# Reciprocal roots of three layer normalisations: a power on POOL in place of a guessed start and Newton steps

## The chip, the cores and the metric

The kernel runs on one core of a Trainium2 chip. The metric is the device time of one execution in microseconds. The kernel before was run three times: median 2804.71 us, lowest 2804.29, highest 2805.34.

## The reference

A decoder layer in fp32 on x of shape (2, 2048, 512): three sublayers, each a layer normalisation followed by a residual branch.

```python
def _layernorm(x, axis=-1, eps=1e-05):
    m = jnp.mean(x, axis=axis, keepdims=True)
    v = jnp.var(x, axis=axis, keepdims=True)
    return (x - m) / jnp.sqrt(v + eps)

x = x + attn(_layernorm(x), W_q, W_k, W_v, W_o)   # 16 heads of 32, rotary positions, softmax
h = gelu(_layernorm(x) @ ctx^T)                    # ctx_1024: 77 rows of 512, per batch
x = x + h @ ctx
w = (weights >= 0) * 2 - 1                         # 512 x 512
x = x + clip((_layernorm(x) @ w^T) * scale + bias, -100, 100)
```

What matters here is `1 / sqrt(v + eps)`: one number per row of x and per normalisation, 3 x 4096 in all. In the kernel a row lies on a partition, so for one chunk of 128 rows it is a tile of one column.

## The kernel before

A batch has 2048 rows: 16 chunks of 128 rows, or 4 blocks of 4 chunks. Each of the two batches goes through two stages.

**Projection** (`project_batch`, L153). For each chunk: `norm` computes mean and variance on DVE (`chunk_stats`: bn_stats L129, bn_aggr L130 into the tile mv), the reciprocal root, and on ACT the scaled chunk xn = x * rstd + off (L168) with off = -mean * rstd. `turn` transposes xn on PE (pt, L174) and copies it to xnt on ACT (L176). PE then multiplies xnt with the three weights (pk, pq, pv, all L181), DVE and POOL rotate k and q (L209 to L214; the last addition of r is POOL's), and PE transposes them (ptqk, L189). The normalisation of chunk ch + 1 is written ahead of the products of chunk ch. Input chunks and weights come by DMA from the SP queue (L71, L76).

**Attention** (`Attention.run`, L595). A batch has 32 units (a block of queries, a group of four heads, a half block), and a unit 8 steps. In each half of a step PE computes scores (st, L516) and, for a unit ahead, scores for the row maxima (ps, L423); ACT takes the exponential (pw, L643); POOL adds two halves of it (sm, L645); DVE reduces the maxima (L435). PE weighs the values (acc, L534) one step later and sums sm with a matrix of ones (acc, L548) two steps later. In this stage the order on PE, DVE, ACT and POOL is the order of the program (`tc.manual_schedule`); elsewhere a planner orders the instructions of each engine. After a unit's last step ACT copies acc to num (L562), DVE takes a reciprocal (L568) and a product gives the attention output (L571), which overwrites q.

**After attention** (`after_attention`, L284) is a generator that handles 4, 2 or 1 chunks of a block ("a piece"): output projection (po, L329) and residual addition on DVE (L298), a normalisation, the context branch (ph L336, the gelu steps L341 to L350, po L355), a second normalisation, and the last branch (pf, L363, then y: L365 on DVE, L367 to L370 on POOL) and the store (L372). Every `yield` ends one slot. Pieces stand in a first-in first-out queue. `background` (L380) runs one slot after one half of every second step and after the second half of every step (L654, L663); in the last four units of a batch it runs one in each half (L652). During the next projection it runs three at a time, and `drain` empties the queue before that projection's last block. When all attention is done, the rest runs alone (`alone` is set), one slot of each piece in turn.

**The normalisation** is in both places three parts. `rstd_seed` (L133) makes v = var + eps on DVE and a first guess of the root by shifting and subtracting the bits as an integer (L138, L139). `rstd_step` (L144) is one Newton iteration of four dependent small instructions (L145 to L148), run three times on POOL. Then two instructions make off (L165, L166 or L311, L312). Inside `after_attention` the iterations and off go to `side()`, which is POOL, or DVE once the kernel is alone; a slot ends after the seed, after each iteration and, twice, after off. In `project_batch` there are no slots. The small tiles (mv, v, rstd, t, off) have two buffers each (pool `small`, L63).

The lines that the change touches and those that call them:

Of the kernel before, what the change touches and what calls it, by code (L numbers as in the profile page):

```python
# [8 lines left out]

F32 = mybir.dt.float32  # L10
BF16 = mybir.dt.bfloat16
U32 = mybir.dt.uint32
I32 = mybir.dt.int32
AF = mybir.ActivationFunctionType
ALU = mybir.AluOpType
AX = mybir.AxisListType

P = 128
# [6 lines left out]
CPB = BLK // P  # L25
# [6 lines left out]
EPS = 1e-5  # L32
# [5 lines left out]
def decoder_layer(  # L38
# [16 lines left out]
    nc = tc.nc  # L55

    const = ctx.enter_context(tc.tile_pool(name="const", bufs=1))
# [5 lines left out]
    small = ctx.enter_context(tc.tile_pool(name="small", bufs=2))  # L63
# [31 lines left out]
    nc.vector.memset(ones_b, 1.0)  # L95
    ones = const.tile([P, DK], F32, tag="ones", name="ones")
    nc.vector.memset(ones, 1.0)


    mts = []  # L100
# [26 lines left out]
    def chunk_stats(xc, mv):  # L127
        st = small.tile([P, 6], F32, tag="st", name="st")
        nc.vector.bn_stats(st, xc)  # L129
        nc.vector.bn_aggr(mv, st)  # L130


    def rstd_seed(var, n):  # L133
        v = small.tile([P, n], F32, tag=f"v{n}", name="v")
        nc.vector.tensor_scalar(v, var, 1.0, EPS, ALU.mult, ALU.add)
        y = small.tile([P, n], F32, tag=f"rstd{n}", name="rstd")
        t = small.tile([P, n], F32, tag=f"t{n}", name="t")
        nc.vector.tensor_scalar(t.bitcast(I32), v.bitcast(I32), 1, None, ALU.arith_shift_right)  # L138
        nc.vector.tensor_scalar(  # L139
            y.bitcast(I32), t.bitcast(I32), -1.0, float(0x5F3759DF), ALU.mult, ALU.add  # L140
        )
        return v, y, t

    def rstd_step(engine, v, y, t):  # L144
        engine.tensor_mul(t, y, y)  # L145
        engine.tensor_mul(t, t, v)
        engine.tensor_scalar(t, t, -0.5, 1.5, ALU.mult, ALU.add)
        engine.tensor_mul(y, y, t)  # L148

# [1 line left out]
    def project_batch(b, ahead, att, wk, wq, wv):  # L153

        def norm(ch):
            xc = ahead.pop(0)
            if ch + 2 < NCH:
                ahead.append(load_x(b, ch + 2))
            mv = small.tile([P, 2], F32, tag="mv1", name="mv")
            chunk_stats(xc, mv)  # L160
            v, y, t = rstd_seed(mv[:, 1:2], 1)
            for _ in range(3):
                rstd_step(nc.gpsimd, v, y, t)
            off = small.tile([P, 1], F32, tag="off1", name="off1")
            nc.gpsimd.tensor_mul(off, mv[:, 0:1], y)  # L165
            nc.gpsimd.tensor_scalar(off, off, -1.0, None, ALU.mult)  # L166
            xn = work.tile([P, D], F32, tag="w", name="xn")
            nc.scalar.activation(xn, xc, AF.Identity, bias=off, scale=y)  # L168
            return xn

        def turn(xn):
            pt = ps_t.tile([P, ND, P], F32, tag="t", name="pt")
            for i in range(ND):
                nc.tensor.transpose(pt[:, i, :], xn[:, i * P : (i + 1) * P], ident)  # L174
            xnt = work.tile([P, ND, P], F32, tag="w", name="xnt")
            nc.scalar.copy(xnt, pt)  # L176
            return xnt

        def times(dst, xnt, w, part=range(ND)):
            for i in part:  # L180
                nc.tensor.matmul(dst, xnt[:, i, :], w[:, i, :], start=(i == 0), stop=(i == ND - 1))  # L181

        def transpose_qk(ch, qk, which=(0, 1)):
            blk, c = divmod(ch, CPB)
            cols = slice(c * P, (c + 1) * P)
            for a in which:
                pt = ps_s.tile([P, ND, P], F32, tag="s", name="ptqk")
                for i in range(ND):
                    nc.tensor.transpose(pt[:, i, :], qk[:, a, i * P : (i + 1) * P], ident)  # L189
                (nc.vector.tensor_copy if a else nc.scalar.copy)((att.q, att.k)[a][blk][:, :, cols], pt)  # L190
            if c == CPB - 1 and 1 in which:
                att.open_block(blk)

        def values(ch, xnt, pool=None):
            pv = (pool or ps_s).tile([P, D], F32, tag="t" if pool else "s", name="pv")
            times(pv, xnt, wv)
            v = kvq.tile([P, D], F32, tag=f"v{ch}", name=f"v_{b}_{ch}")
            nc.scalar.copy(v, pv)  # L198
            att.v.append(v)


        def rotate(ch, a, ps, r):
            half = [P, H, DK // 2]
            cs = cos[:, ch, None, :, None].to_broadcast(half + [2])
            sn = sin[:, ch, None, :].to_broadcast(half)
            pairs = ps.rearrange("p (h i t) -> p h i t", i=DK // 2, t=2)
            t1 = r[:, 0, a, :].rearrange("p (h i t) -> p h i t", i=DK // 2, t=2)
            t2 = r[:, 1, a, :].rearrange("p (h i t) -> p h i t", i=DK // 2, t=2)
            nc.vector.tensor_tensor(t1, pairs, cs, ALU.mult)  # L209
            nc.vector.scalar_tensor_tensor(  # L210
                t2[:, :, :, 0], pairs[:, :, :, 1], -1.0, sn, ALU.mult, ALU.mult
            )
            nc.vector.tensor_tensor(t2[:, :, :, 1], pairs[:, :, :, 0], sn, ALU.mult)  # L213
            nc.gpsimd.tensor_add(r[:, 0, a], r[:, 0, a], r[:, 1, a])  # L214

        xnt = turn(norm(0))
        held = None
        for ch in range(NCH):
            if ch == (NB - 1) * CPB:
                drain()  # L220
            blk, c = divmod(ch, CPB)
            if c == 0:
                att.q.append(kvq.tile([P, ND, BLK], F32, tag=f"q{blk}", name=f"q_{b}_{blk}"))
                att.k.append(kvq.tile([P, ND, BLK], F32, tag=f"k{blk}", name=f"k_{b}_{blk}"))
            r = big.tile([P, 2, 2, D], F32, tag="s", name="r")
            xn = norm(ch + 1) if ch + 1 < NCH else None
            pk = ps_t.tile([P, D], F32, tag="t", name="pk")
            pq = ps_t.tile([P, D], F32, tag="t", name="pq")
            if ch == NCH - 1:
                break  # L230
            times(pk, xnt, wk)
            rotate(ch, 1, pk, r)
            att.lead(1)
            background(3)
            times(pq, xnt, wq)
            rotate(ch, 0, pq, r)
            if held is not None:
                transpose_qk(*held)
            held = (ch, r[:, 0])
            xnt_next = turn(xn)  # L240
            if ch < NCH - 2:
                values(ch, xnt)
            else:
                left = xnt
            att.lead(1)
            background(3)
            xnt = xnt_next


        times(pk, xnt, wk)  # L250
        rotate(ch, 1, pk, r)
        transpose_qk(*held)
        values(ch - 1, left, ps_t)
        transpose_qk(ch, r[:, 0], (1,))
        for i in range(ND):
            times(pq, xnt, wq, (i,))
            att.lead(1)
        rotate(ch, 0, pq, r)
        att.lead(2 * AHEAD)
        values(ch, xnt, ps_t)  # L260
        transpose_qk(ch, r[:, 0], (0,))
        att.split_maxima(0)
        att.turn_maxima(0)
        att.key_steps()
# [5 lines left out]
    def side():  # L270
        return nc.vector if alone else nc.gpsimd
# [12 lines left out]
    def after_attention(b, blk, ot, first, end):  # L284
        wo, wf, fs, fb = late["wo"], late["wf"], late["fs"], late["fb"]
        ctxn, ctxt = late["ctx"]
        n = end - first
# [14 lines left out]


        def norm(mv):
            v, y, t = rstd_seed(mv[:, :, 1], n)
            yield False
            for _ in range(3):
                rstd_step(side(), v, y, t)
                yield False
            off = small.tile([P, n], F32, tag=f"off{n}", name="off")  # L310
            side().tensor_mul(off, mv[:, :, 0], y)  # L311
            side().tensor_scalar(off, off, -1.0, None, ALU.mult)  # L312
            yield False
            yield False
            for c in range(n):
                xn = work.tile([P, D], F32, tag="w", name="xn2")
                nc.scalar.activation(
                    xn, xs[c], AF.Identity, bias=off[:, c : c + 1], scale=y[:, c : c + 1]
                )
                yield True  # L320
                pt = bank([P, ND, P], "pt2")
                for i in range(ND):
                    nc.tensor.transpose(pt[:, i, :], xn[:, i * P : (i + 1) * P], ident)  # L323
                nc.scalar.copy(ot[:, :, chunks[c]], pt)
                yield c + 1 == n
# [5 lines left out]
        mv = small.tile([P, n, 2], F32, tag=f"mv{n}", name="mv2")  # L331
# [25 lines left out]
        mv = small.tile([P, n, 2], F32, tag=f"mv{n}", name="mv3")  # L357
# [375 lines left out]
```

## Time and profile before

| what | us |
|---|---|
| median of three runs | 2804.71 |
| the profiled execution, its own time | 2803.13 |
| its span | 2801.0 |
| PE busy (matmuls) | 2762.5 |
| POOL busy | 1804.3 |
| DVE busy | 1714.5 |
| ACT busy | 1319.9 |
| PE matmuls on the chain that ended last | 96% of the span |

The span runs from the first to the last instruction of one profiled execution. Busy times of different engines overlap. The 2.1 us between the span and that execution's own time lie around the span. In the stages: the first projection lasts until about 228 us, the first attention until 1368, the second projection until about 1620, the second attention until 2752, and what runs alone until 2801.

### The profile page before, as it was taken

The numbers are of one execution on the slowest core, as the hardware profiler recorded it, in microseconds if no ns is written. First come the engines' busy times: TensorE is split into PE (matmuls) and PEld (weight loads), VectorE is DVE, ScalarE is ACT, GpSimd is POOL, SyncE is SP. The second block draws the span as 40 slices with busy tenths as digits, with TensorE's granted clock in tenths as the row PEclk, the third lists the DMA queues.
The fourth block names the chain that finished last, engine by engine and source line by source line (L and its number), as shares of the span: only waits on it lengthen the run. The fifth ranks groups of instructions, "written<-read, shape, count | busy, mean of one in ns | idle before, by whom it ended". The sixth has DMA issues, their size and how long they took to land.

```text
span 2801.0 us, 70846 instructions
## 1 busy us (share of the span) xinstructions
PE 2762.5 (99%) x30748; PEld 1490.8 (53%) x30748; DVE 1714.5 (61%) x3003; ACT 1319.9 (47%) x2391; POOL 1804.3 (64%) x2393
## 2 busy tenths in 40 slices
PE   8999999999999999999999999999999999999997
PEld 4445555555555555555444455555555555555553
DVE  4436777666666766665244467766766666666644
ACT  1114555455546544654322155555555455545542
POOL 4326767567757685767644287766777566857772
PEclk9999999999999999999999999999999999999998
DMA  4000000000100010000201000000000000000000
GB/s 136 20 19 2 5 4 4 4 4 7 30 3 4 4 33 4 4 4 33 72 24 31 15 4 4 4 4 4 4 17 20 4 4 11 26 4 4 18 11 16
DMA packets 41864, 43.56 MB, mean 16 GB/s; under 512 B 24759, under 2 KB 24759, under 8 KB 41553
## 3 DMA queue, kind: packets, MB, share of 16 engines
q1 hardware_dynamic: 41552, 39.05, 4.7%
q8 instruction: 240, 3.93, 0.6%
q14 instruction: 72, 0.58, 0.1%
HBM read 26.58 MB, written 8.39 MB: 12 GB/s over the span
## 4 chain that ended last, share of the span: by engine, by line
PE 96%; DVE 2%; POOL 1%; issue 1%; ACT 0%; DMA 0%; ACTq 0%; DVEq 0%; POOLq 0%
PE st L516 21%; PE acc L534 21%; PE ps L423 18%; PE acc L548 8%; PE pf L363 4%; PE pk L181 4%; PE po L329 4%; PE pv L181 4%; PE pq L181 4%; PE st L501 3%; PE pt L323 1%; PE po L355 1%; PE ph L336 1%; PE ptqk L189 1%; PE pt L174 1%
## 5 line engine op out<-in xcount | busy, mean ns | idle before, releaser
L645 POOL TENSOR_TENSOR sm<-pw 128x512 f32<-128x512 f32 x1024 | 1297.6, 1271 | 628.4 <-ACT pw L643 624.2
L435 DVE TENSOR_REDUCE mx<-ps 128x1 f32<-128x512 f32 x2048 | 1311.8, 682 | 566.6 <-PE ps L423 563.9
L643 ACT ACTIVATE pw<-st 128x512 f32<-128x512 f32 x2048 | 1111.3, 595 | 1004.0 <-PE ps L423 665.9
L423 PE MATMUL ps<-k,q 32*128 32x512 f32 x4096 | 1221.6, 639 | 2.2 <-ACT v L198 1.1
L534 PE MATMUL acc<-pw,v 128*32 128x256 f32 x8192 | 655.6, 391 | 0.0
L548 PE MATMUL acc<-sm,ones 128*32 128x128 f32 x7680 | 392.2, 280 | 1.4 <-POOL sm L645 1.4
L423 PEld LDWEIGHTS ps<-k,q 32*128 32x128 f32 x4096 | 359.4, 183 | 46.7 <-issue 24.3
L534 PEld LDWEIGHTS acc<-pw,v 128*32 128x32 f32 x8192 | 162.4, 108 | 402.3 <-issue 383.2
L548 PEld LDWEIGHTS acc<-sm,ones 128*32 128x32 f32 x7680 | 248.7, 110 | 157.2 <-POOL sm L645 2.7
L516 PE MATMUL st<-q,dkq 32*128 32x256 f32 x2048 | 291.4, 401 | 0.0
L516 PE MATMUL st<-q,dkk 32*128 32x256 f32 x2048 | 291.0, 400 | 0.0
L516 PE MATMUL st<-q,dkv 32*128 32x256 f32 x2048 | 289.9, 400 | 0.0
L516 PE MATMUL st<-q,k 32*128 32x256 f32 x2048 | 265.5, 375 | 0.0
L516 PEld LDWEIGHTS st<-q,dkk 32*128 32x128 f32 x2048 | 175.4, 184 | 90.1 <-issue 48.0
L516 PEld LDWEIGHTS st<-q,dkq 32*128 32x128 f32 x2048 | 172.2, 184 | 79.9 <-issue 55.2
L516 PEld LDWEIGHTS st<-q,dkv 32*128 32x128 f32 x2048 | 174.7, 184 | 68.8 <-issue 37.3
L516 PEld LDWEIGHTS st<-q,k 32*128 32x128 f32 x2048 | 194.4, 187 | 13.6
L214 POOL TENSOR_TENSOR r<-r 128x512 f32<-128x512 f32 x64 | 81.0, 1267 | 184.6 <-DVE r L213 167.0
L568 DVE RECIPROCAL num<-num 128x128 f32<-128x128 f32 x128 | 120.5, 943 | 64.2 <-ACT num L562 64.2
L190 ACT COPY q<-ptqk 128x512 f32<-128x512 f32 x32 | 18.9, 590 | 222.6 <-PE ptqk L189 222.6
L181 PE MATMUL pk<-wk,xnt 128*128 128x512 f32 x256 | 119.7, 611 | 2.7 <-ACT xnt L176 2.7
L363 PE MATMUL pf<-wf,q 128*128 128x512 f32 x256 | 119.1, 609 | 0.0
(99 smaller groups left out, 1963.9 us busy)
## 6 DMA issues: line engine op xcount, KB each, us to landing
x<-in_x_dram SPq DMA_DIRECT2D x64, 256.0 KB, 2.7
out_dram<-x SPq DMA_DIRECT2D x32, 256.0 KB, 2.0
wk<-in_wk_t_dram SPq DMA_DIRECT2D x2, 1024.0 KB, 5.3
wq<-in_wq_t_dram SPq DMA_DIRECT2D x2, 1024.0 KB, 8.0
wv<-in_wv_t_dram SPq DMA_DIRECT2D x2, 1024.0 KB, 12.9
wo<-in_wo_t_dram SPq DMA_DIRECT2D x1, 1024.0 KB, 7.0
wf<-in_wf_t_dram SPq DMA_DIRECT2D x1, 1024.0 KB, 9.1
mrow<-mt SPq DMA_TRANSPOSE x62, 2.3
```

What stands on the lines that cost most here:

```text
L181: nc.tensor.matmul(dst, xnt[:, i, :], w[:, i, :], start=(i == 0), stop=(i == ND - 1))
L329: nc.tensor.matmul(ps, ot[:, i, cols], wo[:, i, :], start=(i == 0), stop=(i == ND - 1))
L363: nc.tensor.matmul(pf, ot[:, i, cols], wf[:, i, :], start=(i == 0), stop=(i == ND - 1))
L423: nc.tensor.matmul(ps, self.q[qb][self.rows[h], g, q0 : q0 + P], self.k[kb][self.rows[h], g, :], start=True, stop=True,)
L435: nc.vector.tensor_reduce(mx[:, qc, h, kb : kb + 1], ps, AX.X, ALU.max)
L501: nc.tensor.matmul(self.st[h], ones_b[r, :], mrow[r, None, :].to_broadcast([DK, 2, HQ]), start=True, stop=False, skip_group_check=True,)
L516: nc.tensor.matmul(self.st[h][:, c, :], keys[r, g, kc * P : (kc + 1) * P], self.q[qb][r, g, hf * HQ : (hf + 1) * HQ], start=False, stop=Tr ...
L534: nc.tensor.matmul(acc[self.rows[h], 0, :], self.v[self.chunk(i, c)][:, d0 : d0 + DK], pw[:, h, c, :], start=(i == 0 and c == 0), stop=(i ...
L548: nc.tensor.matmul(acc[self.rows[h], 1, part], ones, sm[:, h, part], start=False, stop=(i == STEPS - 1), skip_group_check=True,)
L568: nc.vector.reciprocal(num[:, 1, part], num[:, 1, part])
L643: nc.scalar.activation(pw[:, h], self.st[h], AF.Exp, scale=SCALE)
L645: nc.gpsimd.tensor_add(sm[:, hs, :], pw[:, hs, 0, :], pw[:, hs, 1, :])
```

## The change

The seed and the three Newton iterations go. The new helper `scale_and_shift` adds eps on the given engine, raises the sum to the power -0.5 on POOL with a constant tile of -0.5, and makes off on the given engine as before. Both `norm` functions call it: the projection with POOL; the pieces with `side()`, so with POOL, or with DVE around the one POOL instruction once the kernel is alone. In a piece all of it is in one slot, followed by the two yields that stood after off. For one normalisation that leaves 4 small instructions of 17, and 2 slots of 6.

```diff
+    minus_half = const.tile([P, CPB], F32, tag="minus_half", name="minus_half")
+    nc.vector.memset(minus_half, -0.5)
...
-    def rstd_seed(var, n):
-        v = small.tile([P, n], F32, tag=f"v{n}", name="v")
-        nc.vector.tensor_scalar(v, var, 1.0, EPS, ALU.mult, ALU.add)
+    def scale_and_shift(engine, mv, n):
         y = small.tile([P, n], F32, tag=f"rstd{n}", name="rstd")
-        t = small.tile([P, n], F32, tag=f"t{n}", name="t")
-        nc.vector.tensor_scalar(t.bitcast(I32), v.bitcast(I32), 1, None, ALU.arith_shift_right)
-        nc.vector.tensor_scalar(
-            y.bitcast(I32), t.bitcast(I32), -1.0, float(0x5F3759DF), ALU.mult, ALU.add
-        )
-        return v, y, t
-
-    def rstd_step(engine, v, y, t):
-        engine.tensor_mul(t, y, y)
-        engine.tensor_mul(t, t, v)
-        engine.tensor_scalar(t, t, -0.5, 1.5, ALU.mult, ALU.add)
-        engine.tensor_mul(y, y, t)
+        engine.tensor_scalar(y, mv[:, :, 1], EPS, None, ALU.add)
+        nc.gpsimd.tensor_tensor(y, y, minus_half[:, :n], ALU.pow)
+        off = small.tile([P, n], F32, tag=f"off{n}", name="off")
+        engine.tensor_mul(off, mv[:, :, 0], y)
+        engine.tensor_scalar(off, off, -1.0, None, ALU.mult)
+        return y, off
...
-            mv = small.tile([P, 2], F32, tag="mv1", name="mv")
-            chunk_stats(xc, mv)
-            v, y, t = rstd_seed(mv[:, 1:2], 1)
-            for _ in range(3):
-                rstd_step(nc.gpsimd, v, y, t)
-            off = small.tile([P, 1], F32, tag="off1", name="off1")
-            nc.gpsimd.tensor_mul(off, mv[:, 0:1], y)
-            nc.gpsimd.tensor_scalar(off, off, -1.0, None, ALU.mult)
+            mv = small.tile([P, 1, 2], F32, tag="mv1", name="mv")
+            chunk_stats(xc, mv[:, 0])
+            y, off = scale_and_shift(nc.gpsimd, mv, 1)
...
         def norm(mv):
-            v, y, t = rstd_seed(mv[:, :, 1], n)
-            yield False
-            for _ in range(3):
-                rstd_step(side(), v, y, t)
-                yield False
-            off = small.tile([P, n], F32, tag=f"off{n}", name="off")
-            side().tensor_mul(off, mv[:, :, 0], y)
-            side().tensor_scalar(off, off, -1.0, None, ALU.mult)
+            y, off = scale_and_shift(side(), mv, n)
             yield False
             yield False
```

More of the change, by code (lines that the diff above doesn't have):

```diff
@@ L11 @@
 BF16 = mybir.dt.bfloat16
-U32 = mybir.dt.uint32
-I32 = mybir.dt.int32
 AF = mybir.ActivationFunctionType
```

## The prediction

> **What bounds the kernel now.** I read the page's head first, then a table of busy time by stage, TensorE's waits, the chain at both ends, and the groups of the instructions concerned.
>
> ```profile
> span 2801.0 us, 70846 instructions
> PE 2762.5 (99%) x30748; PEld 1490.8 (53%) x30748; DVE 1714.5 (61%) x3003; ACT 1319.9 (47%) x2391; POOL 1804.3 (64%) x2393
> ```
>
> PE is busy 2762.5 of 2801.0 us. No arithmetic of PE changes, so the change can only move the 38.5 us in which PE is idle, the matmuls at half clock, or POOL far enough to become the bound. By stage (length, then each engine's busy us):
>
> ```profile
> 0.00:11.00 11.00, 0.26 (x1) 0.26 (x2) 2.83 (x15) 2.10 (x2) 4.89 (x34) 1.00 0.80 248
> 230.00:1340.00 1110.00, 1109.73 (x14286) 616.25 (x14284) 737.52 (x1189) 596.79 (x1090) 785.18 (x879) 1.00 0.03 9
> 1340.00:1372.00 32.00, 27.66 (x335) 15.90 (x326) 7.26 (x25) 17.23 (x31) 23.85 (x61) 1.00 0.33 108
> 1372.00:1620.00 248.00, 244.03 (x797) 113.59 (x797) 104.64 (x247) 46.97 (x78) 108.20 (x281) 1.00 0.09 26
> 2751.60:2801.00 49.40, 32.26 (x88) 15.23 (x88) 28.00 (x110) 7.57 (x14) 0.00 (x0) 0.82 0.06 21
> ```
>
> PE's idle time sits at the start (10.7), between the batches (4.3), in the second projection (4.0) and after the last attention (17.1); attention itself leaves 0.3. What PE waits for:
>
> ```profile
> PE pt L174 <- ACT xn L168: 13.2, 3, 10.7
> PE pt L323 <- ACT xn L317: 8.7, 3, 5.6
> ```
>
> Both are the scaled chunk, the last link of a normalisation. The chain at the start (start, us, what):
>
> ```profile
> 4.37 0.18 DVE mv L130
> ...
> 9.88 0.82 ACT xn L168
> ...
> 12.53 6.49 PE pk L181 x8
> ```
>
> and at the end, where two one-chunk pieces, A and B, run side by side:
>
> ```profile
> 2755.59 3.45 PE po L329 x8
> ...
> 2764.41 0.17 DVE mv L130
> ...
> 2769.75 0.82 ACT xn L317
> ...
> 2780.72 0.17 DVE mv L130
> ...
> 2783.93 0.82 ACT xn L317
> ```
>
> The removed steps, of which L145 stands for four lines:
>
> ```profile
> L145 POOL TENSOR_TENSOR t<-rstd x150: 187/194/207, 5.7 to 2741.7; 128x1 f32<-128x1 f32 x96, 128x4 f32<-128x4 f32 x36, 128x2 f32<-128x2 f32 x18
> L145 DVE TENSOR_TENSOR t<-rstd x12: 151/159/160, 2761.3 to 2783.0; 128x1 f32<-128x1 f32 x12
> ```
>
> **What the Trainium skill says.** GPSIMD Engine Reference, Performance pitfalls: a chain of dependent fp32 operations costs 4 cycles a step at 1.2 GHz; its Specifications give each of eight cores 16 lanes and 16 partitions, so one column of a tile is one vector. No page prices the power, and no row of the trace has one. Perfetto Trace Analysis, GPSIMD Engine Instruction: POOL's times are better read from start to start. Here L145 lasts 0.19 but dependent steps are 0.27 apart; I use 0.27 on POOL and 0.19 on DVE. TensorE: Matmul & The Clock Gate, Part 1: TensorE starts at half clock; the trace agrees (first pk 6.49 us, later ones 3.43).
>
> **Cost of the power.** From below: any small two-input step, 0.27 us. Estimate from the skill's 4 cycles: a logarithm and an exponential of about 50 dependent steps (my assumption) are 200 cycles, 0.17 us a column; with the fixed 0.27 about 0.5 for one column and 1.0 for four. From above: the 16 lanes one after another, 16 x 0.17 = 2.6 us a column, 10.6 for four. I take 0.5 and 1.0. The range keeps both ends.
>
> **The change, part by part.** (1) *Start.* The aggregate ends at 4.55. Then a 0.09 hop, add 0.27, power 0.5, product 0.27, negation 0.26: ACT starts at 5.9 instead of 9.88, and pk could start at 8.6. But wk must have landed. wq was issued at 2.11 and took 10.9 us (13.0), wv 2.66 and 12.9 (15.6), so 2.6 us per weight matrix, and wk about 10.4. Gain 12.53 - 10.4 = 2.1 (0 to 3.9). If wk was early, the whole 3.9 shows.
>
> (2) *Attention.* 12 normalisations of four columns and 6 of two run on POOL. Each loses 3 DVE seeds and 12 POOL steps of 0.27 and gets an add, a power and the same two last steps, all in one slot. That slot is 0.27 + 1.0 + 0.27 + 0.27 = 1.8 us where three had 1.1 each and a fourth 0.5. Queued behind it are the sm additions (L645), for which PE's row sums wait; but a step's sums are taken two steps later, and a step is (1368.2 - 227.6) / 256 = 4.46 us. This slack hides it: 0. DVE's seeds were hidden as well. POOL's add now waits for DVE's aggregate, given a slot (about 2 us) before it: 0.
>
> (3) *Between batches.* POOL runs the first two normalisations of the second batch between the last sm additions (1348 to 1354), then a piece's L145-L148 steps; from 1351 to 1361 the chain alternates between sm and these steps, and PE waits. Of the 4.34 us idle, 2.1 (pt L174 for xn, then pk for xnt) stand behind the last num copy and stay; of the other 2.2 I take 2.0.
>
> (4) *Second projection.* PE idles 1.10 in 1415-1420 and 1.58 in 1465-1470, where POOL is busy 4.75 and 3.92 of 5 us with interleaved Newton steps. 16 instead of 48 steps there: 2.0 of the 2.7. The rest of the 4.0 also stands in the first projection, and stays. DVE's waits for a free mv (68.9 us, 21 times) shrink; PE covers them. The wait for a free rstd passes from DVE (10.3 us) to POOL's add, with the r additions behind it: covered.
>
> (5) *Tail.* Every normalisation also loses four yields. The queue is first in, first out, so the last four-chunk piece ends 8 slots sooner and the two-chunk piece after it (queued near 2600.7, begun at 2672.2) 16 sooner. It overhung attention by 7 slots (pt, pf, pf and their y steps), so all of it moves inside. PE is full there: +0.44 + 2 x 3.44 = +7.3. In return, from the end of the last acc (2751.6): po starts when the first q is divided (2753.6), not at 2755.4: 1.8. B's addition no longer waits for DVE (2762.46 to 2762.94): 0.5. B's first normalisation, aggregate to ACT, is 5.2 now, as it is interleaved with A's 17 steps and y; it becomes 0.19 + 0.1 + 0.5 + 0.1 + 2 x 0.19 = 1.3: 3.9. The second 3.0 becomes 1.3: 1.7. And A, one po (3.4) ahead of B, can run its pf under B's normalisation; I take half: 1.7. Net 9.6 - 7.3 = 2.3.
>
> Sum 2.1 + 2.0 + 2.0 + 2.3 = 8.4. The profiled execution took 2803.1 (span 2801.0 and 2.1 around it): 2794.7. The runs' median is 1.6 above it: 2804.7 - 8.4 = 2796.3.
>
> **Rivals.** *Covered:* wk lands only just before 12.5, A and B stay coupled, and the gaps of (3) and (4) half remain: 0 + 1 + 1 + 0.6, so 2802. For it: the landing of wk isn't shown, and the moved 7.3 us nearly cancel the tail. Against it: several independent gaps would all have to stay. *The first power loads its code:* GPSIMD Engine Reference, Instruction dispatch, has about 6 us for the first call of a freshly loaded kernel. Here it would fall on the start's chain: ACT at about 11.9, 2.0 later than now, total 8.4 - 2.1 - 2.0 = 4.3, 2800. Nothing in the trace speaks to it. *POOL becomes the bound (slower):* with lanes in turn a four-column slot holds POOL 10.6 + 0.8 us against 4.5 of slack: 12 x 6.9 + 6 x 1.6 = 92 us of PE waiting in L548 for sm; start and tail lose 3 x 2.1 of their gain. About 2804.7 + 92 - 2 = 2895. It decides from about 4.3 us for four columns, where 12 x (4.3 + 0.8 - 4.5) = 7 eats the sum. Against it: vector lanes; for it: no measured power. *The change does nothing* can't be: the tail's chain is DVE steps that vanish.
>
> **How the numbers follow.** Forecast 0.68 (own range 2792 to 2801), covered 0.09, code load 0.04, POOL bound 0.19 (anything from 2806 to 2900). About 0.2% (5.6 us) is what can be told from no change: the bounds are 2799.1 and 2810.3. Nine tenths of the forecast is faster, 0.61; its rest, the two middle cases and the cheapest of the slow end 0.20; slower 0.19. 0.05 lie below 2790 and 0.14 above 2822.
>
> **What would show it.** The power's row on POOL: under 1.2 us for four columns, (2) holds; over 4, idle PE at L548. Start: pk's first matmul near 10.4. 1340-1372: PE idle near 2.3. The last two-chunk piece's pf before the last acc, po 2 us after it, and from last acc to the end about 37 us instead of 46.4. It is wrong if POOL's power is several microseconds, or if the shifted pieces meet another full engine (y on POOL is 4.5 us a chunk) inside attention.

## The result, and the profile after

The changed kernel takes 2784.42 us (median of six runs, 2783.80 to 2785.53) against 2804.68 for the kernel before in its six (2803.58 to 2805.34): a ratio of 0.9928, 95% interval 0.9916 to 0.9941. That is 20.3 us less where 8.4 were forecast, and below the range of 2790 to 2822. The direction and several terms of the sum held; one term priced at nothing was the largest of all, and one priced as a gain was a loss.

The head of the page, kernel after:

```profile
span 2782.8 us, 70154 instructions
PE 2750.7 (99%) x30748; PEld 1491.3 (54%) x30748; DVE 1675.7 (60%) x2792; ACT 1320.4 (47%) x2391; POOL 1756.4 (63%) x1903
```

PE runs the same 30748 matmuls, yet its busy time fell from 2762.5 to 2750.7 us. So 11.8 of the 18.2 us of span were lying inside time that the page had counted as busy. Idle time fell only from 38.5 to 32.1. This is the first thing that the prediction's reading ("the change can only move the 38.5 us in which PE is idle", the matmuls at half clock, or POOL) left out. Half clock isn't where the 11.8 were: the stretches with a granted clock of 0.50, the start aside, sum to 20.4 us before and to 23.1 after.

Busy time by stage, kernel after (stretch, length, then busy us of PE, PEld, DVE, ACT, POOL with instruction counts, granted clock, DMA share, GB/s):

```profile
0.00:11.00 11.00, 2.25 (x6) 1.33 (x7) 2.24 (x10) 3.39 (x4) 2.91 (x14) 1.00 0.75 253
230.00:1340.00 1110.00, 1109.00 (x14329) 619.55 (x14326) 730.02 (x1172) 599.91 (x1095) 782.96 (x823) 1.00 0.03 9
1340.00:1372.00 32.00, 29.93 (x283) 16.10 (x284) 3.44 (x6) 12.66 (x23) 21.76 (x18) 0.95 0.44 149
1372.00:1620.00 248.00, 243.14 (x866) 113.70 (x866) 103.62 (x209) 50.76 (x85) 84.77 (x122) 0.99 0.07 21
2740.00:2782.80 42.80, 28.48 (x148) 14.00 (x136) 17.22 (x46) 9.05 (x17) 5.56 (x7) 0.87 0.03 13
```

Idle PE in 1340 to 1372 went from 4.34 to 2.07 us, in 1372 to 1620 from 3.97 to 4.86. Attention (the second row) shows PE full in both kernels, and can't tell on its own whether it got shorter.

For that, the stages have to be divided where the program's own matmuls begin and end. These times are from the matmul records of the two profiled executions, each border being the start of a matmul: to the first pk; on to the first st of L496 (L516 before); first attention (first st to last row sum); the boundary between the batches with the second projection; second attention; from the last row sum to the end.

| us | to pk | to st | attention 1 | boundary, projection 2 | attention 2 | tail | span |
|---|---|---|---|---|---|---|---|
| before | 12.53 | 215.25 | 1140.03 | 246.48 | 1136.89 | 49.83 | 2801.01 |
| after | 9.86 | 214.44 | 1138.11 | 244.84 | 1137.05 | 38.48 | 2782.78 |

One correction is needed to read it. In each batch the last two-chunk piece now ends inside attention, as predicted: one pt (0.59 us) and two pf (3.63 us each), 7.85 us of PE work, stand before the last row sum where they stood after it. (The 7.85 count each record from its start to its end; from start to start the same matmuls take 7.3, the prediction's figure, so each corrected length is uncertain by some 0.5 us.) If the moved work cost attention all of its own length, the attentions lost 1140.03 - (1138.11 - 7.85) = 9.8 and 1136.89 - (1137.05 - 7.85) = 7.7 us, about 17.5 together; the boundary, which should have lost 7.85 and lost 1.6, got 6.2 longer; the tail got 11.35 - 7.85 = 3.5 shorter net; and the start, with the first projection, gave 2.67 + 0.81 = 3.5. The sum is 18.3, the span's difference but for rounding. Kernels with the same order of work in attention repeat its length within 0.2 us from trace to trace (1137.05, 1137.16 and 1137.18 for the second attention of three of them below), so differences of 1 us there can be read.

The power's row, kernel after, by shape (count, busy us, mean ns of one, idle before it and what ended that):

```profile
L136 POOL TENSOR_TENSOR rstd<-rstd,minus_half 128x1 f32<-128x1 f32 x36 | 20.3, 566 | 21.8 <-DVE rstd L135 19.3 <-DVE off L139 0.4
L136 POOL TENSOR_TENSOR rstd<-rstd,minus_half 128x4 f32<-128x4 f32 x12 | 12.5, 1041 | 1.0
```

0.57 us for one column and 1.04 for four: the estimates were 0.5 and 1.0. The chain at the start, kernel after (start, us, what):

```profile
5.49 1.05 POOL rstd L136 x2
...
7.21 0.82 ACT xn L155
...
9.86 5.67 PE pk L168 x8
```

The first power took no longer than later ones: the 1.05 us are two of them, of the first two chunks, run together. ACT starts at 7.21 and not at 9.88. PE's waits, kernel after (us, times, longest):

```profile
PE pt L161 <- ACT xn L155: 9.5, 2, 8.1
PE pt L303 <- ACT xn L297: 8.1, 5, 3.6
```

The first went from 13.2 to 9.5; its longest, 8.1, is the start. The chain at the end, kernel after:

```profile
2744.68 7.08 PE po L309 x16
...
2753.24 0.19 DVE mv L130
...
2753.69 0.56 POOL rstd L136
...
2754.72 0.82 ACT xn L297
...
2768.44 8.67 PE pf L343 x16
```

The last row sum starts at 2744.30, and po 0.4 us later (before: 4.4 later). From the aggregate to ACT are 1.48 us; piece B's took 5.34 before. The two pieces' pf still run as one block of 16, 8.67 us, after both normalisations.

The chain in the second projection, kernel after:

```profile
1462.86 2.74 DMA x<-in_x_dram
...
1465.62 0.64 DVE st L129
...
1467.64 1.81 PE ps L403 x2
1469.45 6.29 PE pq L168 x8
```

DVE stood waiting for a load of x, the reductions of the scores came behind it, PE paused for 1.61 us, and the next projection group ran at half clock: 6.29 us for 8 matmuls where full ones take 3.43, with a granted clock of 0.50 from 1467.9 to 1474.7. The longest pause of this stage is another one, in which the transpose of a piece waits for its own scaled chunk (PE's timeline):

```profile
1391.38 0.66 PE L303 MATMUL pt<-ident,xn 128*128 128x128 f32 x4 [2.10 <-ACT xn L297]
```

### Where the attention's time was hidden

The groups by shape of the kernel before, for the removed seed's shift on DVE (busy us, mean ns | idle before):

```profile
L138 DVE TENSOR_SCALAR t<-v 128x4 int32<-128x4 int32 x12 | 10.1, 843 | 0.4
L138 DVE TENSOR_SCALAR t<-v 128x1 int32<-128x1 int32 x36 | 5.3, 148 | 0.7
```

Four columns take 0.843 us on average and one takes 0.148. The mean mixes two cases: four of the twelve wide shifts began with no POOL addition under way and took 0.17 us, and the eight others 1.18. So it isn't 0.7 us of arithmetic. The timeline of the kernel before at one of them (start, us, engine, line, what, idle before and what ended it):

```profile
534.56 1.27 POOL L645 TENSOR_TENSOR sm<-pw 128x512 f32<-128x512 f32 x1 [0.74 <-ACT pw L643]
...
534.68 1.18 DVE L138 TENSOR_SCALAR t<-v 128x4 int32<-128x4 int32 x1
...
535.98 1.28 DVE L435 TENSOR_REDUCE mx<-ps 128x1 f32<-128x512 f32 x2
...
536.71 0.18 PEld L423 LDWEIGHTS ps<-k,q 32*128 32x128 f32 x1 [0.42 <-DVE mx L435]
```

The shift begins 0.12 us after a POOL addition and ends at 535.86, just after that addition does (535.83). All eight long ones begin and end so. The reductions mx queue behind the shift, and PE's next weight load for a score waits 0.42 us for one. The Trainium skill describes this: SBUF — State Buffer, section "Who interferes with whom", says that a DVE operation in a two-port mode, `tensor_scalar` among them, and a GpSimd instruction exclude each other for the whole of the one that came first; VectorE: DVE Perf Modes, section "What auto-detection actually checks", gives that mode to one source and a destination in SBUF whose outermost non-unit dims are "both even or equal". The trace agrees with the shape: four columns are held, one is not. In the projections four one-column shifts begin 0.16 to 0.60 us into a POOL addition and last 0.14 to 0.15. The waits of PE's weight loads for mx, before and then after:

```profile
PEld ps L423 <- DVE mx L435: 14.4, 23, 1.4
```

```profile
PEld ps L403 <- DVE mx L415: 6.5, 7, 2.4
```

Most of this doesn't show as idle PE, and I take it to lie in the matmuls' modelled ends, which isn't shown. What is shown is where the busy time fell: the scores' matmuls (ps) were busy 1221.6 us before and 1208.8 after, for the same 4096.

### The profile page after: what moved, and what is told of

Same layout as the page of the kernel before. It is cut to its first block, busy times and chain, and to the rows that moved or that the text cites. A ratio compares the mean times of both kernels' runs of the same rounds, so it can differ in the third digit from the quotient of the medians.

```text
span 2782.8 us, 70154 instructions
## 1 busy us (share of the span) xinstructions
PE 2750.7 (99%) x30748; PEld 1491.3 (54%) x30748; DVE 1675.7 (60%) x2792; ACT 1320.4 (47%) x2391; POOL 1756.4 (63%) x1903
## 4 chain that ended last, share of the span: by engine, by line
PE 97%; POOL 1%; DVE 1%; DMA 0%; ACT 0%; issue 0%; ACTq 0%; POOLq 0%; DVEq 0%
PE st L496 22%; PE acc L514 22%; PE ps L403 18%; PE acc L528 8%; PE po L309 4%; PE pf L343 4%; PE pq L168 4%; PE pk L168 4%; PE pv L168 4%; PE st L481 3%; PE pt L303 1%; PE po L335 1%; PE ph L316 1%; PE ptqk L176 1%; PE pt L161 1%
## 5 line engine op out<-in xcount | busy, mean ns | idle before, releaser
L403 PE MATMUL ps<-k,q 32*128 32x512 f32 x4096 | 1208.8, 640 | 1.6 <-DVE mx L415 1.6
L496 PE MATMUL st<-q,dkk 32*128 32x256 f32 x2048 | 291.1, 400 | 0.0
L496 PE MATMUL st<-q,dkq 32*128 32x256 f32 x2048 | 289.9, 400 | 0.0
L496 PE MATMUL st<-q,dkv 32*128 32x256 f32 x2048 | 289.9, 400 | 0.0
L496 PE MATMUL st<-q,k 32*128 32x256 f32 x2048 | 262.8, 374 | 0.0
L496 PEld LDWEIGHTS st<-q,dkk 32*128 32x128 f32 x2048 | 175.4, 184 | 93.2 <-issue 52.3
L496 PEld LDWEIGHTS st<-q,dkq 32*128 32x128 f32 x2048 | 172.7, 184 | 82.6 <-issue 56.7
L496 PEld LDWEIGHTS st<-q,dkv 32*128 32x128 f32 x2048 | 174.7, 184 | 65.2 <-issue 33.6
L496 PEld LDWEIGHTS st<-q,k 32*128 32x128 f32 x2048 | 195.2, 187 | 14.2
L168 PE MATMUL pq<-wq,xnt 128*128 128x512 f32 x256 | 120.9, 612 | 0.0
## 6 DMA issues: line engine op xcount, KB each, us to landing
wq<-in_wq_t_dram SPq DMA_DIRECT2D x2, 1024.0 KB, 10.5
```

The source lines that it names most:

```text
L403: nc.tensor.matmul(ps, self.q[qb][self.rows[h], g, q0 : q0 + P], self.k[kb][self.rows[h], g, :], start=True, stop=True,)
L496: nc.tensor.matmul(self.st[h][:, c, :], keys[r, g, kc * P : (kc + 1) * P], self.q[qb][r, g, hf * HQ : (hf + 1) * HQ], start=False, stop=Tr ...
```

## The experiments

My theory was by now: *the seeds' wait behind POOL* was in the way of the reductions, and that is most of what attention gained. The rivals: *fewer POOL instructions* (12 Newton instructions for each of 16 normalisations in the two attentions), *fewer slots* (the pieces' work earlier), and *fewer DVE instructions* as such.

### The seeds put back beside the power

The changed kernel, with the three seed instructions run on DVE and their result unused. Three kernels differ in w alone, the columns that the seeds work on: w is n (4 or 2) in the first kernel, n - 1 in the second, 1 in the third.

```diff
         def norm(mv):
+            if not alone:
+                w = n
+                sv = small.tile([P, w], F32, tag=f"sv{n}", name="sv")
+                ss = small.tile([P, w], F32, tag=f"ss{n}", name="ss")
+                nc.vector.tensor_scalar(sv, mv[:, :w, 1], 1.0, EPS, ALU.mult, ALU.add)
+                nc.vector.tensor_scalar(ss.bitcast(I32), sv.bitcast(I32), 1, None, ALU.arith_shift_right)
+                nc.vector.tensor_scalar(ss.bitcast(I32), ss.bitcast(I32), -1.0,
+                                        float(0x5F3759DF), ALU.mult, ALU.add)
             y, off = scale_and_shift(side(), mv, n)
```

> The changed kernel with the three DVE seed instructions put back in every piece inside attention, full width (4 or 2 columns), their result unused; slots and POOL's work stay as changed. Theory A1 (the seeds wait on DVE until POOL's addition ends, the reductions behind them come late and PE's ps matmuls wait): the shift instruction again lasts over 0.8 us on average with four columns, and 6 to 14 us of the gain are lost, 2790 to 2798. Theory A2 (the gain in attention comes from fewer slots or less POOL work): at most 2 us are lost, 2784 to 2786.

> As with the seeds put back, but on one column less (3 or 1), so the same number of DVE instructions on an odd count of columns. Theory A1 as a lock (the Trainium skill, SBUF, has a VectorE instruction of a two-port mode[...] wait out a POOL instruction): the seeds last 0.15 us each and at most 3 us are lost, 2784 to 2787. If it is the mere number of DVE instructions ahead of the reductions, the loss is that of the full width.

> The changed kernel with the three DVE seeds put back on one column only, the width at which the seeds lasted 0.15 us each in every run so far; slots and POOL's work as changed. If the cost is the wait behind POOL's addition, the attentions are within 1.5 us each of the changed kernel's (1138.1 and 1137.1). If it is three more instructions ahead of the reductions, they lose 4.5 us each as with three columns (1142.6).

Measured: n columns 2793.77 us (ratio to the kernel before 0.9960, 0.9946 to 0.9974), n - 1 columns 2791.92 (0.9954, 0.9939 to 0.9969), one column 2785.16 (0.9935, 0.9920 to 0.9950). Each ratio is to the kernel before as it ran beside that kernel. By stage, against after: the attentions grew by 5.4 and 5.3 us with n columns, by 4.5 and 4.5 with n - 1, by 1.0 and 1.0 with one. The shift's row by shape, in the kernels with n, n - 1 and one column:

```profile
L299 DVE TENSOR_SCALAR ss<-sv 128x4 int32<-128x4 int32 x12 | 10.0, 835 | 0.4
```

```profile
L299 DVE TENSOR_SCALAR ss<-sv 128x3 int32<-128x3 int32 x12 | 10.0, 835 | 0.4
```

```profile
L299 DVE TENSOR_SCALAR ss<-sv 128x1 int32<-128x1 int32 x18 | 2.7, 152 | 0.6
```

PE's weight loads waiting for mx, with n columns and with one:

```profile
PEld ps L414 <- DVE mx L426: 15.1, 21, 2.6
```

```profile
PEld ps L414 <- DVE mx L426: 8.8, 11, 2.6
```

The instruction count is the same in all three, so *fewer DVE instructions* is worth 2.0 us of the 10.7 at most. The rest, 8.7 us, goes with the wait behind POOL. In the two attentions all seed instructions together last 19.8 us with n columns, 17.4 with n - 1 and 6.9 with one: 12.9 us more of DVE cost 8.7 us of attention, and 10.5 more cost 7.0. So about two thirds of DVE's delay reached PE here.

What holds the shift is seen at the same place in the three kernels. Eight of the twelve wide shifts begin some 0.12 to 0.15 us into a POOL addition, last 1.15 to 1.18 us and end 0.02 to 0.03 us after it, with four columns and with three; with one column, shifts that begin 0.10 to 0.13 us into the addition last 0.15 and are done about 1 us before it is. So three columns wait as four do. The expectation of a free odd count had misread the page: its condition is even *or equal*, and three columns in and three out are equal. That one column falls out of it is my reading of "non-unit dims", and that the hold is exactly that port rule is the page's statement and not a measurement of mine.

The medians hide part of it: with n and n - 1 columns the second projection was 3.3 and 3.5 us shorter than in after. PE pauses there as in after, but is at half clock for 3.4 us and not for 10.2. That stage is taken up below.

### The slots, and POOL's Newton steps, put back

Four empty slots after the normalisation:

```diff
             y, off = scale_and_shift(side(), mv, n)
+            for _ in range(4):
+                yield False
```

> The changed kernel with four empty slots after the power in every piece, so that the pieces take as many slots as before. Theory A1: inside attention nothing is lost; the end of the two-chunk pieces falls behind attention again, and by the sum of the prediction the tail then loses 2 us; the second projection gets back part of its 5.9 us: 2780 to 2787. Theory A2 (fewer slots make the gain in attention): 8 us or more are lost, above 2792.

And the same slots with the twelve POOL instructions in them. Their result, t, is not used; they are there for their time:

```diff
             y, off = scale_and_shift(side(), mv, n)
+            yield False
+            for _ in range(3):
+                if not alone:
+                    t = small.tile([P, n], F32, tag=f"t{n}", name="t")
+                    nc.gpsimd.tensor_mul(t, y, y)
+                    nc.gpsimd.tensor_mul(t, t, y)
+                    nc.gpsimd.tensor_scalar(t, t, -0.5, 1.5, ALU.mult, ALU.add)
+                    nc.gpsimd.tensor_mul(t, y, t)
+                yield False
```

> The changed kernel with four more slots after the power, as in the run with the slots put back, and in three of them the twelve small POOL instructions of the Newton steps (their result unused); DVE's seeds stay away. If the seeds on DVE are what cost PE time in attention, the two attentions stay within 2 us each of the run with empty slots (1131.8), and the time is 2776 to 2781. If POOL's Newton steps are the cost, the attentions lose 4 us each or more, and the time is above 2784.

Measured: 2776.70 us (0.9899, 0.9884 to 0.9913) and 2776.93 (0.9905, 0.9890 to 0.9919). Both are *faster* than after, the first more so than the 2780 to 2787 expected. The last two-chunk piece again ends outside attention, so their stages compare with before directly: the empty slots' attentions are 1131.77 and 1131.77, which is 8.3 and 5.1 us below before. That 13.4 us is what the shorter normalisation gives attention with its slots kept: 10.7 from the seeds, if their cost is the same here as with the slots dropped; 1.8 from POOL's steps (1.85 in the first attention, -0.06 in the second, the steps' attentions less the empty slots'); 0.9 left over. So *fewer POOL instructions* counts little. (The two medians are alike although the steps cost 1.8: with the steps the first pk of the second batch took 3.70 us at full clock, with empty slots 5.40 at half clock.)

With the slots dropped, the attentions are 1138.11 - 1131.77 = 6.3 and 5.3 us longer, with 7.85 of moved work in each. The 4.1 us between these 11.6 and 15.7 are also the 4.1 between 17.5 and 13.4: either the moved work filled time in which PE would have stood, or fewer slots gained something. Which, no run tells.

Dropping the slots was a loss as a whole. Against the kernel with empty slots it cost those 11.6 us in the attentions, and it gave back only 4.3 in the tail, which lost the 7.85 of moved work, and nothing in the boundary and second projection, which lost as much work and became 1.1 longer; the start and first projection are 1.1 shorter. Together 7.3 of span. In the tail, the pf left over after attention fills time that PE would otherwise stand idle; moved inside, it lengthens a full stage.

### POOL's slack

The changed kernel with four more powers behind each of the pieces' in attention (unused results), and the kernel before with all its Newton steps in one slot:

```diff
             y, off = scale_and_shift(side(), mv, n)
+            if not alone:
+                for _ in range(EXTRA):    # EXTRA is 4
+                    more = small.tile([P, n], F32, tag=f"more{n}", name="more")
+                    nc.gpsimd.tensor_tensor(more, y, minus_half[:, :n], ALU.pow)
```

> The changed kernel with four more powers after each normalisation of a piece inside attention (result unused): POOL's slot grows from 1.8 us to about 6 with four columns and 4 with two. By the slack of the prediction (4.46 us of delay of the sm additions is free) a slot of 6 us costs PE about 1.5 us in each of 12 normalisations, up to 18 us in all: 2786 to 2803. If row sums have more slack than that: within 2 us of 2784. If POOL has no slack: 12 x 4.2 + 6 x 3 = 68 us, 2850.

```diff
             v, y, t = rstd_seed(mv[:, :, 1], n)
-            yield False
             for _ in range(3):
                 rstd_step(side(), v, y, t)
-                yield False
```

> The kernel before, with the seed, the three Newton steps and off of a piece in one slot, so four slots fewer and no power. If the seeds cost the time in attention and fewer slots cost it in the second projection, nothing is gained: with the two-chunk pieces inside attention 1140 + 7.5 = 1147 per attention, tail 40 to 43, and the time is 2800 to 2812. If fewer slots are the gain, it is below 2797.

Measured: 2808.94 us (1.0016, 1.0008 to 1.0025), above the 2786 to 2803 expected, and 2826.36 (1.0080, 1.0063 to 1.0097), above 2800 to 2812. PE's waits, first kernel and second:

```profile
PE acc L533 <- POOL sm L630: 14.9, 12, 1.4
```

```profile
PE pt L321 <- ACT xn L315: 24.2, 11, 5.6
```

With four more powers (4.2 us more of POOL for four columns, a slot of about 6) the attentions grew by 10.9 and 9.6 us. Ten of the twelve four-column normalisations make PE wait 1.4 us each for the sums sm, about 7 us after the first power; a two-column one adds two short waits. That is 14.9 of the 20.6 us; the rest isn't traced. So the prediction's slower rival had its mechanism right: POOL's slack, 6.0 us of slot less 1.4 of waiting, is near the 4.5 us it used, and a slow power would have made PE wait at just that line; at 1.04 us it doesn't.

In the second kernel POOL's chain in one slot makes the scaled chunk late for PE's transpose: by 4.2 us at the end of the first attention, 4.1 and 4.2 in the second projection, 3.5 and 5.6 in the tail. Its attentions take 1155.44 and 1143.84 us against 1140.03 and 1136.89 before, with the 7.85 of moved work in each. In after the same two transposes that waited 4.2 and 4.1 us still wait, 1.0 and 2.1; with four empty slots they don't. So a distance of two slots is short even for the power.

### The pieces alone

The changed kernel with the projection's normalisation as before:

```diff
             mv = small.tile([P, 1, 2], F32, tag="mv1", name="mv")
             chunk_stats(xc, mv[:, 0])
-            y, off = scale_and_shift(nc.gpsimd, mv, 1)
+            v, y, t = rstd_seed(mv[:, 0, 1:2], 1)
+            for _ in range(3):
+                rstd_step(nc.gpsimd, v, y, t)
+            off = small.tile([P, 1], F32, tag="off1", name="off1")
+            nc.gpsimd.tensor_mul(off, mv[:, 0, 0:1], y)
+            nc.gpsimd.tensor_scalar(off, off, -1.0, None, ALU.mult)
```

> The pieces have the power, the projections keep the seed and the Newton steps. Theory A (most of the gain is made inside attention, in the pieces): the first st of the first attention is back near 227.6 us (3.5 us lost at the start), the two attentions keep their 14 us, the tail keeps its part; the time is about 2788 to 2791. Theory B (most of the gain comes from the start and the projections): the time is above 2796.

Measured: 2794.30 us (0.9963, 0.9948 to 0.9977), somewhat above the 2788 to 2791 expected. Against after it loses 2.6 at the start, 4.6 in the first attention and 1.5 in the tail; the second attention is the same (1137.18). The 4.6 have one place, in this kernel's timeline of PE:

```profile
1328.42 1.12 PE L327 MATMUL pt<-ident,xn 128*128 128x128 f32 x4 [2.14 <-ACT xn L321]
```

The next batch's first two normalisations hold POOL from 1319.86 to 1324.54 with 28 small steps. The last piece's own normalisation and a sum addition queue behind them, PE waits 2.14 us for its scaled chunk, and the granted clock is 0.74 and 0.57 in the five-microsecond stretches at 1325 and 1330 (0.50 for 6.8 us from 1327.4). In after this transpose waits 1.00 us and the clock stays full there; one such normalisation takes POOL from 1318.49 to 1319.91. So half of the 20 us goes with the projections' normalisations, through the start and this place, and half with the pieces. The 1.5 of the tail stand where no projection runs; there PE was at half clock for 13.7 us, and for 10.2 in after.

### The second projection

`background(n)` sets how many slots of the pieces' work are run at a time there. Five in place of three, at both places where it is called, in the changed kernel; then eight empty slots in place of the four above; then four with five, and eight with five.

```diff
-                    background(3)
+                    background(5)
```

> The changed kernel with five background slots instead of three at each place of a projection, so that the piece in the second projection ends sooner and gives its x buffers back before the chunks need them. If the loss in the second projection (244.8 us, with 7.5 us less PE work in it than before) comes from x loads that wait for the piece's stores, DVE's waits for x shrink from 12.5 us, PE stays at full clock around 1470 and the stage falls to 238 to 241: 2779 to 2782. If it comes from the piece's own chain or is chance of the order, it stays within 1.5 us of 244.8.

> The changed kernel with eight empty slots after the power instead of four. If the overhang of the two-chunk piece is only useful as filling for PE's idle time in the tail, a longer overhang gives up to 2 us more: 2774 to 2777. If the overhanging piece becomes the last chain, the tail grows beyond 45 us: 2778 to 2784.

> The power with four empty slots after it and five background slots at each place of a projection: both of the edits that shortened the changed kernel. If the gains of the two add (the second projection loses 8 us against the run with empty slots, attentions 1131.8), 2769 to 2772. If the five slots only mended the wait near 1465 us, which the empty slots had mended already, the time stays at 2775 to 2778.

> The same with eight empty slots. With gains that add, 2766 to 2770; with a second projection that has no more to give than in the run with four slots (242 to 244 us), 2772 to 2776.

| | median us | ratio to before, 95% | boundary and projection 2, us | PE idle in it | at half clock in it |
|---|---|---|---|---|---|
| after | 2784.42 | 0.9928 (0.9916 to 0.9941) | 244.8 | 6.9 | 10.2 |
| background 5 | 2779.02 | 0.9909 (0.9894 to 0.9924) | 236.8 | 3.2 | 3.4 |
| 4 slots | 2776.70 | 0.9899 (0.9884 to 0.9913) | 235.9 | 3.2 | 3.4 |
| 8 slots | 2774.28 | 0.9894 (0.9877 to 0.9910) | 237.1 | 3.1 | 3.4 |
| 4 slots, 5 | 2779.43 | 0.9910 (0.9895 to 0.9925) | 238.1 | 4.9 | 3.4 |
| 8 slots, 5 | 2772.77 | 0.9885 (0.9869 to 0.9902) | 236.0 | 3.1 | 3.4 |
| before | 2804.68 | 1 | 238.6 | 6.0 | 0 |

In the third column 7.85 us are taken off where the piece's end stands outside attention, so that all compare (with eight slots one more pt, 0.6 us, stands outside and is still in). The last two columns are from the same traces: the time in which no matmul runs, and the time with a granted clock of 0.50. They account for the stage: less the idle time and half of the half-clock time (an estimate of what a clock of 0.50 costs), every row comes to 231.0 to 232.8 us. So every one of these plans removes the loss of after in this stage by removing its pauses. The two long ones, a piece's transpose waiting 2.10 us for its scaled chunk and the scores' of 1.5 to 1.7 us for the reductions, stand in the three kernels with the seeds put back too, and in none with more slots or background 5.

The gains don't add, since either edit alone has removed the pauses: four slots with background 5 came out above both of its expectations, and has a new pause of 1.69 us for the reductions. DVE's waits for x between 1355 and 1625 don't rank the kernels: 12.5 us in after, 9.9 with background 5, 6.5 with four slots, 4.8 before. Why the clock stays at half for 3.4 us behind some pauses and for 6.8 behind others is open. The fastest kernel run, eight empty slots with background 5, takes 2772.8 us, 11.7 less than the change as made.

## Why the prediction was wrong, by its own steps

- **"PE's 38.5 idle us, the matmuls at half clock, or POOL": wrong.** 11.8 us came out of PE's busy time. A busy share of 1109.73 in 1110 was read as "nothing to gain".
- **Price of the power (0.5 and 1.0): right**, 0.57 and 1.04. With it the rival of a code load fell (the first power took no longer than others), and the slower rival, whose slack the added powers bore out.
- **(1) Start, 2.1: right, a little small.** pk came at 9.86, not 10.4, so wk lands by then: 2.67. ACT started at 7.21 and not 5.9, since POOL takes the second chunk's addition, which waits for its aggregate until 5.28, ahead of the first chunk's power. In the kernel with one-column seeds pk waited 1.2 us for wk, which landed at 10.2, so the limit that the prediction named is near. 0.8 more came in the first projection.
- **(2) Attention, "DVE's seeds were hidden as well": the step that failed.** Predicted 0; the attentions lost 13.4 us with the slots kept, and about 17.5 by the account with the slots dropped. Of it 1.85 at the end of the first attention belong to (3). The seeds are 10.7, since each wide shift that meets a POOL addition lasts until its end, with the reductions and then PE behind it; 0.9 has no cause shown, and what the other 4.1 are stays open. The step rested on idle times only: it did not read L138's row by shape, where 843 against 148 ns stood, and left out what DVE and POOL share. POOL's steps and the slack were judged rightly: putting the steps back cost 1.85 us in the first attention and nothing in the second.
- **(3) Between batches, 2.0: right.** Idle 4.34 to 2.07 in 1340 to 1372, "near 2.3" predicted; the first batch's attention alone lost with POOL's steps put back, as this step would have it. The same stretch then lost 1.7 at half clock, counted under (4).
- **(4) Second projection, 2.0 gained: wrong in sign**, 6.2 lost. The two pauses that the step named (1.10 and 1.65 us before) did go. Two others came, of 2.10 and 1.61 us, so idle time rose by 0.9; and PE was at half clock for 10.2 us where it had been at full clock throughout, which is 5.1 us by the estimate above: a pk of 5.39 us (3.70 before) and a pq of 6.29 (3.43) are 4.6 of them. Both new pauses go with the plan of slots (no kernel with more slots or background 5 has them), and a load of x stands before the second. The step priced the pauses that would go and did not ask what is late next, nor what a pause costs beyond its own length.
- **(5) Tail, net 2.3: right in sum, 3.5.** The piece moved inside attention as said (7.85, 7.3 predicted), and B's normalisation fell from 5.34 to 1.48 (1.3 predicted). po gained 4.0 where 1.8 were given. The 1.7 for A's pf under B's normalisation didn't come: the pf still run together. The prediction's "46.4" is a slip: 2801.0 - 2751.6 is 49.4, so its own 9.6 led to 39.8; from the end of the last acc it is 38.1. What it didn't ask is whether the shift is worth having: with the four slots kept, the tail gains 7.0.

In sum: 3.5, 17.5, -6.2 and 3.5 stand where 2.1, 2.0 (with attention's 0), 2.0 and 2.3 stood.

## What to carry to other kernels

Read small instructions by shape, on every engine: one that lasts several times its narrower form may be waiting inside its own duration, as here, and the queue behind it pays. "Busy 99%" of an engine with few buffers behind it doesn't mean that nothing can be gained there; compare the length of the stage between the program's own first and last matmul, and correct it for work that crossed its border. When a step gets shorter and its slots are dropped, price the dropped slots apart, and ask which consumer now comes too soon behind its producer: here the shorter step alone with its old slots was 7.7 us better than both together.

## What I had not expected of the hardware

A 128x4 or 128x3 shift on DVE lasted 0.17 us where it met no POOL addition, and 1.15 to 1.18 us where it began just inside one of 1.27 us; a 128x1 shift lasted 0.15 there. Put back with the rest of the seeds at four and two columns, these cost PE 10.7 us in 2275. POOL's power cost 0.57, 0.73 and 1.04 us for one, two and four columns, about 0.16 for each further column, and the first was no longer than others. And a pause of PE of 1.61 us was followed by 6.8 us at a granted clock of 0.50, in which a group of eight matmuls took 6.29 us in place of 3.43: more lost than the pause itself.
